# A fixed TensorE order for Layer 1 of a gated two-layer block, with ScalarE copies out of PSUM and one softmax inversion a sequence

## The chip, the core and the metric

The kernel runs on one core of a Trainium2 chip. TensorE (PE in the profile) multiplies matrices and leaves the results in PSUM, eight banks of 2 KB a partition; VectorE (DVE), ScalarE (ACT) and GpSimd (POOL) do the rest. GpSimd does not touch PSUM here. SyncE (SP) issues most of the DMAs. Each engine works through its own queue in the order in which the built program holds it, and waits at an instruction whose semaphores have not come.

The metric is the device time of one launch in microseconds (us). Lower is better.

## The reference

Eight sequences of 256 rows and 512 features, x[8, 256, 512], go through two layers. Each layer adds a gated attention and then a gated feed-forward part:

```python
x = x + tanh(g_xattn[0]) * attn0(layernorm(x), ctx, ctx)        # 16 heads of 32, causal
x = x + tanh(g_ffn[0])   * ffn0(layernorm(x))                   # ternary weights, silu(gate)*up, rms norm
x = x + tanh(g_xattn[1]) * attn1(layernorm(x), ctx)             # projections, rms-normed q and k
x = x + tanh(g_ffn[1])   * ffn1(layernorm(x))                   # 8-bit activations, ternary weights
```

What matters for this change is the softmax, `softmax(q k^T) v` for each of 16 heads over 256 keys (text context is empty at this length, so Layer 1 attends to the image context alone), and Layer 1's feed-forward part:

```python
h = rms_norm(x) * w_norm
value, gate = split(act_quant(h) @ weight_quant(w_gv).T)         # 2 x 2048 columns
u = value * silu(gate)
out = x + act_quant(u) @ weight_quant(w_out).T
```

## The kernel before, in words

**Stages.** The program has three stretches. In the first, Layer 0's weights are made ternary while the keys and values of Layer 1 are computed for all sequences and stored in DRAM, and the first two sequences go through Layer 0's attention. In the second, Layer 0's feed-forward part (`Feed0`, lines 645 to 744) runs sequence by sequence; around it are laid the attention of the later sequences, the quantizing of Layer 1's weights, and the first steps of Layer 1's attention. In the third (lines 900 to 1071) Layer 1 is finished: `Attention1` for each sequence and `Feed1` for each half of a sequence (128 rows, called first and second).

**Attention.** A sequence's 16 heads are worked in four groups of four (g = 0 to 3). `scores(g)` multiplies q by k with queries on partitions, and VectorE takes the row maxima `nm`, one reduction for each pair of heads (L329 in Layer 1). `shift` splits the negated maxima into three bf16 parts on GpSimd, turns them with TensorE (`nt`) and copies them to `nT`. `exps(g)` multiplies k by q with keys on partitions, adds the maxima by a second matmul with `sel`, and ScalarE takes the exponential in two halves, `p[1]` first (L400). `weigh(g)` multiplies p by v, and p by `ones`, into the two halves of one PSUM bank `o`; VectorE then inverts the second half (L422) and multiplies (L423), so that `oT` holds finished head outputs. Layer 1 adds the output projection `proj` (L255, reached through `done`).

**Layer 1's feed-forward part.** `norm` (a chain through VectorE and GpSimd) makes 8-bit rows `zq`, a DMA transposes them to `zT`. Each of eight `glu(k)` a half fills one of two `gu` banks with 8 matmuls (L985); ScalarE takes tanh of the first half of the bank (L993), and VectorE reads the bank twice (L994, L996). Only then is the bank free. Every second one is followed by a maximum (L998). `quantize` turns the maxima into a scale, ScalarE scales (L1020), GpSimd rounds (L1021), two DMAs transpose, and `project` multiplies by the output weights into `py` (L1035, added at L1045).

**PSUM in the third stretch.** Score and transpose tiles share a pool `s` of two tiles of two banks each; then there are one `o`, two `gu` and one `py`. Queries' projection, output projection and `project` all use `py`.

**What sets the order.** Every job is a list of steps with a time interval; `timeline` sorts the steps by these times and emits them. The tile framework then schedules each engine's queue itself, by its own model of time, within the dependencies. Inside one `scores` or `exps` the class `Row` ties each matmul behind the one before; otherwise TensorE's order is the scheduler's.

Of the kernel before, what the change touches and what calls it, by code (L numbers as in the profile page):

```python
# [47 lines left out]
P = 128  # L49
# [20 lines left out]
LAG = 2  # L70


@with_exitstack
def flamingo_kernel(
# [104 lines left out]
    for g in range(DC):  # L179
        nc.vector.tensor_copy(sel[:, g, :], chosen[:, g : g + 1].broadcast_to([P, P]))  # L180
    mz = []
    for k in range(2):
        mz.append(const.tile([P, 2, P], BF, name=f"mz{k}"))
        nc.gpsimd.memset(mz[k], 0.0)

# [31 lines left out]

    class Row:
# [4 lines left out]
        def matmul(self, *args, **kwargs):  # L223
            ins = nc.tensor.matmul(*args, **kwargs)  # L224
            if self.last is not None:
                tc.add_manual_dep(
                    ins.ins,
                    self.last.ins.name,
                    mybir.DependencyInfo(
                        mybir.DependencyClass.NoSync, mybir.DependencyReason.DATA  # L230
                    ),
                    reason="row",
                )
            self.last = ins
# [9 lines left out]
    def turned(srcs, dst):  # L244

        t = pair((P, 2, DC, P), name="turned")
        for i, src in enumerate(srcs):
            for c in range(DC):
                nc.tensor.transpose(t[:, i, c, :], src[:, c * P : (c + 1) * P], ident)  # L249
        nc.scalar.copy(dst.rearrange("p c (i t) -> p i c t", i=2), t)  # L250

    def linear(dst, srcT, i, w):

        for c in range(DC):
            nc.tensor.matmul(  # L255
# [8 lines left out]
    class Attention:  # L264
# [68 lines left out]
        def shift(self):  # L333
# [4 lines left out]
            for k in range(MP):  # L338
# [12 lines left out]
                src = rest  # L351
            t = pair((P, 2, P), BF, name="nt")
            for q in range(2):
                nc.tensor.transpose(t[:, q, :], self.mz[:, q, :], ident_b)
# [48 lines left out]
        def weigh(self, g, p):  # L403
# [3 lines left out]
            for k in range(2):  # L407
                for kb in range(2):
                    for r in range(4):
                        h = 4 * g + r  # L410
                        nc.tensor.matmul(  # L411
                            o[HD * r : HD * (r + 1), k, q0[kb] : S],
                            lhsT=ones if k else self.v[:, kb, h * HD : (h + 1) * HD],
# [5 lines left out]
            if g == 0:  # L419
                self.oT = self.new("oT", [DC, S], bufs=1)  # L420
            w = self.new("w", [S])
            nc.vector.reciprocal(w, o[:, 1, :])  # L422
            nc.vector.tensor_tensor(self.oT[:, g, :], o[:, 0, :], w, ALU.mult)  # L423

        def looks(self):
            return self.counted(
                self.nready, [*(lambda g=g: self.scores(g) for g in range(DC)), self.shift]
            )

        def step(self, g):  # L430
            before = getattr(self, "p", None)
            if g < DC:
                self.exps(g)
            if g > 0:
                self.weigh(g - 1, before)

        def weighs(self):
            return self.counted(
# [686 lines left out]
```

## Time and profile before

| | us |
|---|---|
| median of 3 timed runs | 1401.51 (1391.04 to 1401.55) |
| the profiled execution | 1398.44 |
| its span on the core | 1396.6 |
| TensorE busy | 1212.5 (87%) |
| VectorE busy | 900.2 (64%) |
| ScalarE busy | 515.9 (37%) |
| GpSimd busy | 491.0 (35%) |
| mean granted TensorE clock | 0.933 |

"Busy" is the sum of an engine's instructions in the span. A row of the costliest groups has the line, engine and operation, the tiles written and read, the shapes, how many there were, their busy time and the mean duration of one, then how long the engine stood idle before them and what ended that. Windows of the trace give the same busy times for a stretch, with the clock granted to TensorE (1.00 is full speed). The trace's time runs from the start of the span.

### The profile page before, as it was taken

How to read it: one execution, taken by the hardware profiler on the slowest of the kernel's cores; microseconds unless marked ns; L12 is line 12 of the kernel's file. 1: busy time of each engine (PE TensorE's matmuls, PEld its weight loads, DVE VectorE, ACT ScalarE, POOL GpSimd, SP SyncE). 2: the span in 40 equal slices, each digit the busy share in tenths (PEclk: the TensorE clock that was granted, in tenths of full speed). 3: DMA queues.
4: the chain of work that ended last, by engine and by line, in shares of the span. 5: the costliest groups of instructions: out<-in, count | busy, mean ns of one | idle time of the engine just before them, and what ended most of it. 6: DMA issues, size and time to landing. Idle time of an engine off the chain costs nothing.

```text
span 1396.6 us, 28443 instructions
## 1 busy us (share of the span) xinstructions
PE 1212.5 (87%) x11730; PEld 797.8 (57%) x11730; DVE 900.2 (64%) x1913; ACT 515.9 (37%) x978; POOL 491.0 (35%) x744
## 2 busy tenths in 40 slices
PE   5999964879999878999999998979797979898985
PEld 2444432657777656778777774545444545455552
DVE  2758779535656575656556464786858595868673
ACT  2445454555343313343333432323231414142432
POOL 2233242232424779142424234250505050413141
PEclk9999985979999989999999998989899998999998
DMA  6334334672100464101000013212020111111122
GB/s 233 136 129 145 128 107 153 223 196 93 27 32 17 145 208 118 32 17 32 17 32 17 2 62 109 50 31 54 23 61 17 38 43 35 42 28 27 36 46 53
DMA packets 103826, 104.34 MB, mean 75 GB/s; under 512 B 63376, under 2 KB 74640, under 8 KB 103696
## 3 DMA queue, kind: packets, MB, share of 16 engines
q1 hardware_dynamic: 100672, 97.54, 24.0%
q10 hardware_dynamic: 3024, 4.98, 1.1%
q8 instruction: 92, 1.51, 0.4%
q14 instruction: 38, 0.31, 0.1%
HBM read 72.09 MB, written 15.73 MB: 63 GB/s over the span
## 4 chain that ended last, share of the span: by engine, by line
PE 39%; DVE 20%; POOL 8%; ACT 6%; DMA 6%; issue 5%; SPq 0%; ACTq 0%; POOLq 0%; DVEq 0%
PE gu L682 9%; PE s L224 6%; PE o L411 6%; PE y L707 5%; PE gu L985 4%; PE lin L255 4%; DVE nm L329 3%; DMA w<-in_gvT_dram 2%; PE py L1035 2%; DVE ln_st L198 2%; ACT u L1020 2%; DVE t L994 2%; POOL rs_r L191 1%; POOL q L805 1%; PE turned L249 1%
## 5 line engine op out<-in xcount | busy, mean ns | idle before, releaser
L682 PE MATMUL gu<-xT,gu 128*128 128x128 f16 x4096 | 268.2, 224 | 10.0 <-DVE h L692 7.0
L682 PEld LDWEIGHTS <-gu 128*128 128x128 bf16 x4096 | 243.0, 101 | 52.2 <-issue 31.2
L985 PE MATMUL gu<-gv,zT 128*128 128x256 fp8e4 x1024 | 145.5, 292 | 38.1 <-DVE u L996 34.6
L707 PE MATMUL y<-pr,hs 128*128 128x512 f32 x512 | 157.6, 426 | 8.7 <-DVE x L740 4.3
L993 ACT ACTIVATE t<-gu,back 128x256 f32<-128x256 f32 x128 | 59.4, 471 | 262.6 <-PE gu L985 240.3
L985 PEld LDWEIGHTS <-zT 128*128 128x128 bf16 x1024 | 103.2, 104 | 92.1 <-issue 73.3
L191 POOL TENSOR_TENSOR rs_r<-rs_t,mhalf 128x1 f32<-128x1 f32 (+1 forms) x88 | 55.6, 639 | 274.9 <-DVE rs_t L189 200.8
L422 DVE RECIPROCAL w<-o 128x256 f32<-128x256 f32 x64 | 112.3, 1754 | 59.2 <-PE o L411 59.2
L699 POOL TENSOR_TENSOR acc<-acc,h 128x256 f32<-128x256 f32 x112 | 82.7, 738 | 158.0 <-ACT h L697 139.2
L400 ACT ACTIVATE p<-s 128x768 f32<-128x768 f32 (+1 forms) x128 | 109.9, 908 | 24.4 <-PE s L224 15.8
L691 DVE SCALAR_TENSOR_TENSOR h<-h,gu 128x256 f32<-128x256 f32 x128 | 53.3, 416 | 100.5 <-ACT h L690 98.9
L224 PE MATMUL s<-qT,kT 32*128 32x256 f32 (+1 forms) x1024 | 102.9, 405 | 10.2 <-ACT p L400 10.2
L707 PEld LDWEIGHTS y<-pr,hs 128*128 128x128 f32 x512 | 89.6, 196 | 24.3 <-issue 6.5
L694 ACT CAST hs<-h 128x256 fp32r<-128x256 f32 x128 | 51.6, 404 | 140.0 <-DVE h L692 139.8
L1021 POOL TENSOR_SCALAR uq<-u 128x1024 bf16<-128x1024 f32 x32 | 33.4, 1044 | 183.0 <-ACT u L1020 102.1
L1035 PE MATMUL py<-ou,uT 128*128 128x512 fp8e4 x256 | 70.3, 430 | 21.2 <-DVE x L849 12.2
L994 DVE SCALAR_TENSOR_TENSOR t<-t,gu 128x256 f32<-128x256 f32 x128 | 52.1, 413 | 55.7 <-ACT t L993 55.4
L216 POOL TENSOR_TENSOR hs<-h,hs 128x256 fp32r<-128x256 f32 x64 | 46.8, 731 | 114.7 <-ACT hs L694 114.7
L224 PE MATMUL s<-kT,qT 32*128 32x256 f32 (+1 forms) x1024 | 81.4, 393 | 6.3 <-DVE nm L329 4.3
L697 ACT ACTIVATE h<-h 128x256 f32<-128x256 f32 x112 | 46.4, 416 | 92.6 <-POOL hs L216 64.3
L690 ACT ACTIVATE h<-gu 128x256 f32<-128x256 f32 x128 | 48.2, 377 | 84.7 <-PE gu L682 79.9
L224 PEld LDWEIGHTS s<-qT,kT 32*128 32x128 f32 x1024 | 54.0, 199 | 44.4 <-issue 21.8
(142 smaller groups left out, 2133.4 us busy)
## 6 DMA issues: line engine op xcount, KB each, us to landing
w<-in_gvT_dram SPq DMA_DIRECT2D x32, 512.0 KB, 4.0
w<-in_guT_dram SPq DMA_DIRECT2D x32, 256.0 KB, 2.8
w<-in_outT_dram SPq DMA_DIRECT2D x16, 512.0 KB, 4.0
x<-in_x_dram SPq DMA_DIRECT2D x16, 256.0 KB, 5.5
cT<-in_cxT_dram SPq DMA_DIRECT2D x8, 512.0 KB, 4.8
kT<-in_cxT_dram SPq DMA_DIRECT2D x8, 512.0 KB, 4.2
v<-in_cx_dram SPq DMA_DIRECT2D x8, 512.0 KB, 4.1
vd<-v SPq DMA_DIRECT2D x8, 512.0 KB, 5.0
```

Source lines behind the costliest of these rows:

```text
L191: nc.gpsimd.tensor_tensor(r[:, :n], t[:, :n], mhalf[:, :n], ALU.pow)
L224: ins = nc.tensor.matmul(*args, **kwargs)
L400: nc.scalar.activation(self.p[j], s[j][:, :, 0:n], AF.Exp)
L411: nc.tensor.matmul(o[HD * r : HD * (r + 1), k, q0[kb] : S], lhsT=ones if k else self.v[:, kb, h * HD : (h + 1) * HD], rhs=p[r // 2][:, r % ...
L422: nc.vector.reciprocal(w, o[:, 1, :])
L682: nc.tensor.matmul(gu[:, k, half, :], lhsT=wgu[dc][:, j : j + P], rhs=self.xT[:, i, part * DC + dc, :], start=(dc == 0 and part == 0), sto ...
L699: nc.gpsimd.tensor_tensor(self.acc[i], self.acc[i], sq, ALU.add)
L707: nc.tensor.matmul(self.ys, lhsT=hs[:, part, half, :], rhs=wpr[c][:, half * D : (half + 1) * D], start=(c == 0 and half == 0 and part == 0 ...
L985: nc.tensor.matmul(gu[:, half, :], lhsT=self.zT[:, c, :], rhs=wgv[c][1 - half][:, k * S : (k + 1) * S], start=(c == 0), stop=(c == DC - 1),)
L993: nc.scalar.activation(t, gu[:, 0, :], AF.Tanh, scale=self.back[:, 1:2])
L994: nc.vector.scalar_tensor_tensor(t, t, 1.0, gu[:, 0, :], ALU.add, ALU.mult)
L1035: nc.tensor.matmul(py, lhsT=self.uT[:, c, :], rhs=wout[c // 4][:, c % 4, :], start=(c == 0), stop=(c == HC - 1),)
```

## The change

Four things are changed together.

1. **Softmax sums.** The sums' matmul takes `pick[:, g, :]` instead of `ones`: 32 columns of which only the 8 of group g are one. The sums of the four groups thus fall on different partitions and can be added into one tile. `weigh` no longer inverts or multiplies: ScalarE copies the whole bank `o` (128x512) to `oT`, and from the second group on GpSimd adds the sums. In Layer 0's `done` the sums are turned with the outputs (two more transposes a sequence), inverted as 32 numbers a row, and multiplied in. In Layer 1's `done` one inversion of 128x256 is followed by four matmuls with `spread`, which carry the inverses to all partitions, and two multiplications of 128x512; banks `o` and `py` are used in turn (for the first sequence `o` alone).
2. **The gate's bank.** ScalarE copies each `gu` bank (128x512) to SBUF tiles `gv`, and tanh and both VectorE operations read the copy.
3. **The order.** All matmuls and transposes go through a small class `Tensor`; while `held` is set, each is tied behind the one before. It is set for the third stretch alone. There the steps are placed one by one on a grid of sixteen steps a sequence, one `glu` a step.
4. **Finer steps.** `shift` is split into `parts` (GpSimd) and `shift` (TensorE), `weighs` into eight steps; `load` comes before the queries; `zT` has three buffers instead of two.

```diff
+    class Tensor:
+        held = False
+        last = None
+        def kept(self, ins):
+            if self.held:
+                self.last = behind(ins, self.last)
+            return ins
+        def matmul(self, *args, **kwargs):
+            return self.kept(nc.tensor.matmul(*args, **kwargs))
...
                         pe.matmul(
                             o[HD * r : HD * (r + 1), k, q0[kb] : S],
-                            lhsT=ones if k else self.v[:, kb, h * HD : (h + 1) * HD],
+                            lhsT=pick[:, g, :] if k else self.v[:, kb, h * HD : (h + 1) * HD],
...
-            w = self.new("w", [S])
-            nc.vector.reciprocal(w, o[:, 1, :])
-            nc.vector.tensor_tensor(self.oT[:, g, :], o[:, 0, :], w, ALU.mult)
+                self.oT = self.new("oT", [DC + 2, S], bufs=1)
+                self.sums = self.oT[:, DC, :]
+            behind = DC + (g > 0)
+            nc.scalar.copy(self.oT[:, g : behind + 1 : behind - g], o)
+            if g > 0:
+                nc.gpsimd.tensor_tensor(self.sums, self.sums, self.oT[:, behind, :], ALU.add)
...
+                    pe.transpose(sums[:, i, :], self.sums[:, rows], ident)
+                nc.vector.reciprocal(
+                    inv, sums.rearrange("p i (r g e) -> p i g r e", r=4, g=DC)[:, :, :, :, 0]
+                )
...
+            def invert():
+                nc.vector.reciprocal(self.oT[:, DC + 1, :], self.sums)
+            def divide():
+                for k in range(2):
+                    w = bank(("o", "py")[k if self.b else 0], (P, 2, S), name="inv")
+                    for j in range(2):
+                        pe.matmul(
+                            w[:, j, :],
+                            lhsT=spread[:, 2 * k + j, :],
+                            rhs=self.oT[:, DC + 1, :],
+                            start=True,
+                            stop=True,
+                        )
+                    cols = self.oT[:, 2 * k : 2 * k + 2, :]
+                    nc.vector.tensor_tensor(cols, cols, w, ALU.mult)
+            def add(i):
+                xt = xs[2 * self.b + i]
+                nc.gpsimd.tensor_tensor(xt, xt, rob, ALU.add)
+                t = bank(("o", "py")[i if self.b else 0], name="proj")
+                linear(t, self.oT, i, lambda c: wo[:, c, :])
+                nc.vector.scalar_tensor_tensor(xt, t, tg[:, 1:2], xt, ALU.mult, ALU.add)
...
+            gv = work.tile([P, 2, S], F32, tag="gv", name="gv", bufs=3)
+            nc.scalar.copy(gv, gu)
-            nc.scalar.activation(t, gu[:, 0, :], AF.Tanh, scale=self.back[:, 1:2])
-            nc.vector.scalar_tensor_tensor(t, t, 1.0, gu[:, 0, :], ALU.add, ALU.mult)
+            nc.scalar.activation(t, gv[:, 0, :], AF.Tanh, scale=self.back[:, 1:2])
+            nc.vector.scalar_tensor_tensor(t, t, 1.0, gv[:, 0, :], ALU.add, ALU.mult)
-            nc.vector.tensor_tensor(cols, t, gu[:, 1, :], ALU.mult)
+            nc.vector.tensor_tensor(cols, t, gv[:, 1, :], ALU.mult)
...
+        at(b, *((k, step) for k, step in enumerate(first.glus() + second.glus())))
+        for n, f in ((0, first), (8, second)):
+            quantize, turn0, turn1, project = f.done()
+            at(b, (n + 7.9, quantize), (n + 8.5, turn0), (n + 9, turn1), (n + 13.6, project))
+        if b >= 2:
+            norm, turn, load, lin0, lin1, scale, turn_q = a.ready()
+            at(b - 2, (-2.1, norm), (-0.8, turn), (-0.5, load))
+            at(b - 2, *(((-0.3, lin0), (-0.2, lin1)) if b == 2 else ((0.2, lin0), (1.2, lin1))))
+            at(b - 2, (1.9, scale), (3.6, turn_q))
+            s0, s1, s2, s3, parts, shift = a.looks()
+            at(b - 2, (10.2, s0), (12.2, s1), (13.2, s2), (14.2, s3), (14.9, parts))
+            at(b - 1, (2.1, shift))
         if b >= 1:
+            e0, e1, w0, e2, w1, e3, w2, w3 = a.weighs()
+            n = -0.7 if b == 1 else 2.2
+            at(b - 1, (n, e0), (n + 1, e1) if b > 1 else (n + 0.1, e1))
+            at(b - 1, (4.2, w0) if b > 1 else (n + 0.2, w0))
+            at(b - 1, (5.2, e2), (6.2, w1), (7.2, e3), (8.2, w2), (9.2, w3))
+        invert, divide, add0, add1 = a.done()
+        at(b - 1, (9.9, invert), (10.7, divide), (11.2, add0), (12.7, add1))
+        for n, f in ((11.9, first), (12.9, second)):
+            norm, turn = f.ready()
+            at(b - 1, (n, norm), (n + 1.5, turn))
+    pe.held = True
     timeline(*jobs)
```

In the built program a full sequence of the third stretch stands on TensorE in this order, with one `gate` (8 matmuls) to a step: gate 0, lin0, gate 1, lin1, gate 2, nt, e0, gate 3, e1, turn of the queries, gate 4, w0, gate 5, e2, project of the sequence before, gate 6, w1, gate 7, e3, gate 8, w2, gate 9, w3, gate 10, s0, divide, gate 11, add0, gate 12, s1, add1, gate 13, s2, project, gate 14, s3, gate 15, turn of the rows.

VectorE's queue is still the scheduler's: from the inversion on it holds the reductions of s0, the two multiplications, then mixed the gates' operations, both halves' norm chains, the layer norm of a later sequence, and the reductions of s1, s2 and s3, in this order.

## The prediction

> **What bounds the kernel now.** I read the page first (busy shares, slices), then windows of the trace cut at the last gate of each of Layer 1's sequences, then TensorE's waits in that stretch, the costliest groups, and the order in time.
>
> ```profile
> PE 1212.5 (87%) x11730; PEld 797.8 (57%) x11730; DVE 900.2 (64%) x1913; ACT 515.9 (37%) x978; POOL 491.0 (35%) x744
> ```
> ```profile
> core 0: us, PE busy (x) PEld busy (x) DVE busy (x) ACT busy (x) POOL busy (x), PEclk, DMA share, GB/s
> ...
> 200.00:239.00 39.00, 17.95 (x150) 8.11 (x150) 36.18 (x71) 21.98 (x39) 10.14 (x8) 0.63 0.44 135
> 239.00:845.00 606.00, 559.60 (x7141) 441.88 (x7140) 350.16 (x707) 232.18 (x522) 246.28 (x369) 0.95 0.25 74
> ...
> 996.40:1074.00 77.60, 63.02 (x499) 35.18 (x497) 54.12 (x113) 22.85 (x34) 25.81 (x43) 0.93 0.15 38
> 1074.00:1154.50 80.50, 67.16 (x503) 37.60 (x504) 56.40 (x116) 22.98 (x34) 25.91 (x51) 0.90 0.15 40
> ```
> ```profile
> 1046.00:1078.00 32.00, 22.52 (x151) 12.41 (x144) 30.45 (x62) 3.31 (x7) 17.83 (x33) 0.99 0.08 26
> ```
>
> TensorE is nearly full in Layer 0's body (560 of 606 us); VectorE bounds the last 39 us before it. A full sequence of Layer 1 takes 74.0 us on average: the five stretches from 926.2 to 1296.0, 70.2 + 77.6 + 80.5 + 75.0 + 66.5 = 369.8. On average none of the engines is full there, but the last row shows what an average hides: for 32 us VectorE is busy 30.5 and TensorE 22.5. That is the dense part, from the last inversion to the last score maxima.
>
> ```profile
> PE gu L985 <- DVE u L996: 34.6, 18, 6.0
> PE py L1035 <- DVE x L849: 12.2, 6, 2.4
> ```
> ```profile
> 1045.61 1.76 DVE L422 RECIPROCAL w<-o 128x256 f32<-128x256 f32 x1 [0.45 <-PE o L411]
> ...
> 1073.52 2.35 DVE L329 TENSOR_REDUCE nm<-s 128x4 f32<-128x1024 f32 x2
> ```
>
> The dense part runs from 1045.61 to 1075.87: 30.3 us of VectorE work on end. TensorE's waits (us in total, times, longest) name the same engine.
>
> **The change, part by part.**
>
> *Softmax, start and Layer 0.* Each weighing loses an inversion and a multiplication and gains a copy:
>
> ```profile
> L422 DVE RECIPROCAL w<-o 128x256 f32<-128x256 f32 x64 | 112.3, 1754 | 59.2 <-PE o L411 59.2
> ```
>
> With 0.42 us for L423, 2.18 us go, 8.7 a sequence; Layer 0's end gives back 2 x 0.69 us (128x512 multiplications like L557, 691 ns) and a small inversion. ScalarE's copy of 128x512 lies by the cast of the same size (L537, 579 ns), 0.59 us; it has 22 of 39 us filled at the start. The second sequence's four weighings lie in the 39 us that VectorE bounds: 0 to 8.7 us, I take -6, since a quantizing job ends that stretch. In the body TensorE waits 46 us, about 29 of it for VectorE; against that, 6 x 3 GpSimd sums of 0.74 us (L699) and two more transposes a sequence. Bounds -10 to +8; I take -2, most waits being at handovers.
>
> *Handover.* Divide and both projections of the first sequence share the one bank `o`: matmul, multiply, matmul, multiply, project, add, project in series, where before a single projection started the norm. About 3.5 us later at the first norm; lin0, lin1 and a weighing are done meanwhile: +3.
>
> *The gate's bank.* The copy frees a bank 0.59 us after the last matmul, where before tanh (0.47) and two VectorE operations (2 x 0.42, in VectorE's queue) had to end. The 34.6 us of waits for L996 look like the prize. But 8 of these us are in the last sequence; the long ones (4.75, 5.97, 5.11) stand at the end of the dense part, where TensorE now waits for VectorE elsewhere. In the last sequence it is a gain: 16 gates at 1.25 us and two projects, 27 us against 32: -5. ScalarE gets 16 x 0.59 + 4 x 0.59 = 11.8 us a sequence, on 22.9 of 75.
>
> *The fixed order of a full sequence.* From the order in the program and the trace's times I walk one period. TensorE's groups, start to start at full clock: gate 0.90 x16, lin and add 3.54 x4, project 3.48 x2, exps 1.28 x4, weighings 1.87 x4, scores 1.08 x4, two turns 1.9, nt 0.25; new are the four divide matmuls, each shown as two passes, half the columns of a projection in all: 1.8. Sum 56.
>
> - *w3.* ScalarE's queue has half of e3's exponentials, then quantize's two scalings, which wait for gate 7's maximum, then the other half, gate 8's copy and tanh, and w2's copy, which frees `o`. From gate 7's end: copy and tanh 1.1, VectorE 1.6 + 1.0, scalings 2.37, exponential 1.0, copy, tanh, copy 1.65, together 8.8 us with the hand-offs. TensorE has e3, gate 8, w2 and gate 9: 4.95. Wait 3.9.
> - *Inversion.* After w3 a copy (0.6) and GpSimd's sum (0.74): 1.5 us until VectorE can start.
> - *Dense part.* Its list in VectorE's queue is that of before, less 0.42 (L423), plus two multiplications (1.38) and the add of `project` (0.75), which now stands ahead of s3's maxima: 30.3 + 1.7 = 32.0. The turn of the rows is behind s3's maxima in the pool `s`, so TensorE cannot pass it; its own work in this part is 21.2.
> - *From the turn to e3.* 27.9 us of work; nT 0.4, e1 behind e0's exponentials 1.1, the queries' turn behind both of e1's 2.1.
>
> Period: 6.8 + 3.9 + 1.5 + 32.0 + 27.9 + 3.6 = 75.7, at full clock and without new contention.
>
> *Clock.* The walk has pauses of 3.9 (w3), about 2.6 (s3) and 5 (turn).
>
> ```profile
> 1132.90:1135.30 2.40, 0.03 (x1) 0.00 (x0) 2.19 (x8) 0.47 (x1) 0.60 (x4) 1.00 0.00 0
> 1135.30:1138.70 3.40, 3.38 (x9) 1.29 (x9) 3.40 (x12) 0.00 (x0) 0.53 (x1) 0.53 0.19 39
> ```
>
> A pause of 2.4 us was followed by 3.4 us at about half clock. The Trainium skill (TensorE: Matmul & The Clock Gate, "HAM oscillation") asks for no idle gaps over some 3.4 us. By the rule two pauses cost, by the row three; half clock for 3.4 to 6.8 us loses 1.7 to 3.4 us each, but in the dense part TensorE has slack. I charge w3 1.7 and the turn 2.6: 4.3.
>
> *Two SBUF inputs.* Both VectorE operations of a gate had one input in PSUM (at most 423 ns each); now both lie in SBUF. L216's VectorE form, two SBUF inputs of the same size, has a median of 425 ns, but a mean of 476 and a maximum of 1044. The skill (SBUF — State Buffer, "SBUF: two separate sides") says that such an operation and a GpSimd instruction lock each other out for a whole instruction. By the row ten operations in the dense part cost 0.6 us; by the rule, with GpSimd busy 17.8 of 32 us and an estimated half of its 0.8 us left at each meeting, 2.2. I take 1.0.
>
> A full sequence: 75.7 + 4.3 + 1.0 = 81.0, 7.0 more than before; five: +35. The first stretch has the same dense part but no lin, e0 and e1: +3. The sixth has no scores: +4. The end after the last gate stays 18.6.
>
> Sum: -6 - 2 + 3 + 3 + 35 + 4 - 5 = +32. The profiled execution's own time is 1398.4 (span 1396.6, 1.8 around it), 3.1 below the median of the timed runs; 1398.4 + 32 = 1430.4. I say 1430.
>
> Edits at no cost: `pick` for `ones` has the same shape; `load` earlier and `zT`'s third buffer add no work on a filled queue (SP's transposes follow their norms; were `zT` late, gate 0 would wait out a transpose, some 3 us: a pair took 6.48); parts split from shift stays GpSimd work, 2.8 us before nt, behind two adds of 1.27 us and hidden by lin0 and lin1; uncovered it would hold nt for 5.3.
>
> **The rivals.**
>
> *The order keeps TensorE fed (faster).* The place is w3 and the e-phase: if quantize's scale is ready before e3's exponentials, the 3.9 and 3.6 us go, and with shorter pauses most of the half clock: 75.7 - 7.5 + 1 = 69 a sequence, -25 in all; with -6, -6, +3, -2, 0, -5 that is -41, 1357. It decides at 74 - 8/5, about 72 a sequence. For it: before, TensorE ran 20 us windows without a pause. Against it: the two scalings stand between the exponentials in ScalarE's queue, whoever is early.
>
> *The two halves cancel (no change).* If half clock and locks cost no more than before (74 holds 5 us of half clock already, its waits included), a period is 76 and Layer 0 gains 8: 1398 + 10 + 5 - 8 - 5, about 1400.
>
> *Half clock stays (much slower).* If each of the three pauses brings 6.8 us of half clock onto the path and the locks reach 2.2: 75.7 + 9 + 2.2 = 87, +65 and the rest: 1460.
>
> *The order isn't what it says.* The built program has the sixteen steps; little chance.
>
> **How the numbers follow.** Likeliest (1430, its own range 1415 to 1448): 0.50. Fed: 0.20. Cancel: 0.18. Much slower: 0.12. Changes under 1% can't be told from none here. Range 1365 to 1456; faster 0.20, same 0.18, slower 0.62.
>
> **What would show it.** Right: full sequences of about 80 us; a wait of TensorE before w3 for ScalarE's copy of `o` of some 4 us; the turn of the rows waiting for L329's successor about 5 us; VectorE without a pause for 32 us or more; clock at 0.9. Wrong: sequences under 72 us, a clock near 1.00, or w3 without a wait. I would be wrong too if Layer 0's body, whose order the scheduler has made anew, moved by more than 10 us.

## The result, and the profile after

The changed kernel takes **1452.66 us** (median; 1450.09 to 1453.91) against 1399.83 (1391.04 to 1401.55) for the kernel before in the same session: a ratio of **1.0388, 95% interval 1.0341 to 1.0435**. It is slower. The forecast was 1430 with a range of 1365 to 1456; its sum said +32, and the span of the profiled execution grew by 54.0, from 1396.6 to 1450.6 us. The measured time lies 3.3 us inside the upper end of the range and above the 1415 to 1448 that the prediction gave to its own account.

The page's row of busy times of the changed kernel:

```profile
PE 1226.9 (85%) x11810; PEld 813.8 (56%) x11810; DVE 827.1 (57%) x1837; ACT 626.0 (43%) x1170; POOL 535.9 (37%) x797
```

VectorE lost 73 us of work (900.2 before) and ScalarE took 110 more (515.9 before). TensorE's 80 extra matmuls and its slower clock come to 14 us; the other 40 are time in which TensorE stands. To see where, I cut both spans at the same events (the end of Layer 0's last sum of squares, the start of the first gate half of Layer 1, the end of the last gate half of each sequence):

| stage | before, us | after, us | difference | predicted |
|---|---|---|---|---|
| start and Layer 0, to its last sum of squares | 845.8 | 839.4 | -6.4 | -8 |
| handover, to the first gate half | 19.8 | 47.2 | **+27.4** | +3 |
| first stretch | 60.6 | 53.4 | -7.2 | +3 |
| five full sequences | 369.6 | 387.7 | +18.1 | +35 |
| sixth stretch | 50.4 | 60.7 | +10.3 | +4 |
| last sequence's gates | 32.0 | 43.4 | **+11.4** | -5 |
| tail | 18.4 | 18.8 | +0.4 | 0 |
| sum | 1396.6 | 1450.6 | +54.0 | +32 |

The sign was right and the total lay in the range, but five of the seven terms were off, in both directions. The same stages of the changed kernel by windows (stretch and its length, then busy us and count of each engine, granted TensorE clock, DMA share, GB/s):

```profile
core 0: us, PE busy (x) PEld busy (x) DVE busy (x) ACT busy (x) POOL busy (x), PEclk, DMA share, GB/s
199.00:238.40 39.40, 19.61 (x210) 9.47 (x207) 28.51 (x60) 25.10 (x44) 12.23 (x11) 0.76 0.43 135
238.40:839.40 601.00, 554.33 (x7136) 442.03 (x7135) 304.94 (x677) 246.26 (x548) 262.01 (x390) 0.96 0.25 74
839.40:886.60 47.20, 32.17 (x128) 15.06 (x129) 14.85 (x41) 6.20 (x8) 21.60 (x28) 0.75 0.26 81
1019.90:1097.50 77.60, 65.52 (x507) 38.08 (x506) 50.27 (x107) 35.04 (x54) 27.98 (x45) 0.90 0.15 39
1097.50:1174.70 77.20, 62.99 (x507) 36.97 (x506) 50.20 (x106) 34.62 (x54) 25.02 (x42) 0.92 0.17 37
...
1388.00:1431.20 43.20, 28.69 (x160) 17.50 (x158) 25.66 (x63) 20.14 (x37) 8.70 (x11) 0.76 0.19 43
```

VectorE no longer fills the stretch ahead of Layer 0's body (28.5 of 39.4 us, 36.2 of 39 before), yet Layer 0's body starts only 0.9 us earlier (238.4 instead of 239.3 us): the work taken off VectorE did not come off its length. What ends it now was not tested. In the two full sequences ScalarE is busy 35 us instead of 23, and VectorE 50 instead of 55. Three of the rows have a slow clock, but the start and the handover had one before too (0.63 and 0.74); only at the end is it new, 0.76 where it was 0.95.

TensorE's waits over the five full sequences of the changed kernel (940 to 1327 us; what waited, for what, total, times, longest):

```profile
PE turned L210 <- DVE nm L358: 22.7, 5, 6.7
PE o L207 <- ACT oT L456: 17.4, 5, 3.6
PE s L207 <- DVE rs_t L217: 7.1, 4, 1.8
PE py L207 <- DVE x L922: 6.2, 5, 1.3
PE turned L210 <- ACT p L432: 5.2, 5, 1.0
PE inv L207 <- DVE oT L901: 4.0, 5, 1.3
```

The gates' wait for VectorE is gone from the list. Before it was, in these five sequences:

```profile
PE gu L985 <- DVE u L996: 26.7, 10, 6.0
```

In its place stand the two waits that the prediction had named: the turn of the rows behind the score maxima (4.5 us a sequence, about 5 predicted) and the fourth weighing behind ScalarE's copy (3.5, 3.9 predicted).

The handover of the changed kernel in order of time (start, us, engine, operation; in brackets the idle time before it and what ended it):

```profile
844.95 6.75 PE L207 MATMUL proj<-wo,oT 128*128 128x512 f32 x8 [0.78 <-DVE oT L915]
852.62 3.70 PE L207 MATMUL proj<-wo,oT 128*128 128x512 f32 x8 [0.92 <-DVE x L922]
...
860.99 0.42 DVE L1041 TENSOR_SCALAR zq<-z 128x512 bf16<-128x512 f32 x1
...
864.36 1.51 POOL L239 TENSOR_SCALAR y<-x,ln_mv,rs_r 128x512 f32<-128x512 f32 x2
...
865.18 1.97 PE L210 MATMUL turned<-ident,y 128*128 128x128 f32 x8 [8.86 <-POOL y L239]
...
886.63 1.91 PE L207 MATMUL gu<-gv,zT 128*128 128x256 fp8e4 x16
```

The quantized rows `zq` for the first gate half are done at 861.4, and only their transposing DMA is left. But the order puts the turn of another sequence's rows first, and those rows are normed on GpSimd behind both norm chains: TensorE stands for 8.86 us. Behind the turn stand two steps of exponents, a weighing and both projections; the gate half starts at 886.63. The first projection ran at a granted clock of 0.54 after the waits ahead of it, 6.75 us for the eight matmuls that take 3.70 a moment later.

The end of the changed kernel, in order of time:

```profile
1404.87 6.59 PE L207 MATMUL py<-ou,uT 128*128 128x512 fp8e4 x16 [4.56 <-DMA uT<-uq]
1424.97 5.09 PE L207 MATMUL py<-ou,uT 128*128 128x512 fp8e4 x16 [5.44 <-DVE umax L1082]
1441.53 5.34 PE L207 MATMUL py<-ou,uT 128*128 128x512 fp8e4 x16 [9.72 <-DMA uT<-uq]
```

The first two of these projections wait for their transposed input while gate matmuls of the last sequence stand behind them in the fixed order. (The row of the second names VectorE's maximum, which ended just then; the transpose for it was issued at 1421.68 and takes some 3.2 us to land.) Before, the same two projections stood among the last gates as well, but late enough to wait for nothing:

```profile
1357.01 3.62 PE L1035 MATMUL py<-ou,uT 128*128 128x512 fp8e4 x16
...
1373.15 4.24 PE L1035 MATMUL py<-ou,uT 128*128 128x512 fp8e4 x16
```

### The profile page after: what moved, and what is told of

It is laid out like the page before. It is cut to its first block, busy times and chain, and to the rows that moved or that the text cites. A ratio compares the mean times of both kernels' runs of the same rounds, so it can differ in the third digit from the quotient of the medians.

```text
span 1450.6 us, 28745 instructions
## 1 busy us (share of the span) xinstructions
PE 1226.9 (85%) x11810; PEld 813.8 (56%) x11810; DVE 827.1 (57%) x1837; ACT 626.0 (43%) x1170; POOL 535.9 (37%) x797
## 4 chain that ended last, share of the span: by engine, by line
PE 45%; DVE 17%; ACT 8%; POOL 6%; DMA 5%; issue 3%; ACTq 0%; POOLq 0%; DVEq 0%; SPq 0%
PE gu L207 15%; PE s L207 6%; PE o L207 6%; PE y L207 5%; PE lin L207 4%; DVE nm L358 3%; PE proj L207 3%; PE py L207 3%; DMA w<-in_gvT_dram 2%; ACT p L432 2%; PE turned L210 2%; ACT u L1104 2%; DVE t L1078 1%; DVE ln_st L226 1%; DMA w<-in_outT_dram 1%
## 5 line engine op out<-in xcount | busy, mean ns | idle before, releaser
L207 PE MATMUL gu<-xT,gu 128*128 128x128 f16 x4096 | 269.0, 225 | 17.9 <-DVE h L749 13.2
L1075 ACT COPY gv<-gu 128x512 f32<-128x512 f32 x128 | 74.0, 582 | 203.0 <-PE gu L207 202.9
L207 PE MATMUL y<-pr,hs 128*128 128x512 f32 x512 | 154.2, 422 | 2.7 <-POOL hs L244 2.0
L1078 DVE SCALAR_TENSOR_TENSOR t<-t,gv 128x256 f32<-128x256 f32 x128 | 60.8, 477 | 124.0 <-ACT t L1077 122.8
L459 POOL TENSOR_TENSOR oT<-oT 128x256 f32<-128x256 f32 x48 | 37.9, 789 | 164.7 <-ACT oT L456 164.5
L207 PE MATMUL s<-qT,kT 32*128 32x256 f32 (+1 forms) x1024 | 91.8, 395 | 3.9 <-ACT p L432 3.6
L207 PE MATMUL o<-p,v 128*32 128x256 f32 (+1 forms) x1024 | 67.3, 373 | 26.0 <-ACT oT L456 26.0
L207 PE MATMUL py<-ou,uT 128*128 128x512 fp8e4 x256 | 64.1, 408 | 27.2 <-DMA uT<-uq 14.3
L358 DVE TENSOR_REDUCE nm<-s 128x4 f32<-128x1024 f32 x64 | 76.1, 1216 | 0.5 <-PE s L207 0.5
L207 PE MATMUL lin<-wk,cT 128*128 128x512 f32 x128 | 60.3, 616 | 16.9 <-DMA cT<-in_cxT_dram 16.9
```

The lines of the kernel that those rows point to most:

```text
L207: return self.kept(nc.tensor.matmul(*args, **kwargs))
L358: nc.vector.tensor_reduce(nm, s[j].rearrange("p r (q k) -> p r q k", q=2), AX.X, ALU.max, negate=True)
L459: nc.gpsimd.tensor_tensor(self.sums, self.sums, self.oT[:, behind, :], ALU.add)
L1075: nc.scalar.copy(gv, gu)
L1078: nc.vector.scalar_tensor_tensor(t, t, 1.0, gv[:, 0, :], ALU.add, ALU.mult)
```

## The experiments

The ratios are to the kernel before, timed in the same session (its medians there: 1396.2 for the first four runs, 1395.2 for the next four, 1398.5 for the three after them, 1397.3 for the last). None leaves out a part of the reference. The question was whether the loss comes from the fixed order, from ScalarE's copy or from the new softmax; then, which places of the order; then, whether they add up.

### The order not held

```diff
-    pe.held = True
     timeline(*jobs)
```

> The changed kernel with the hold taken off: the sixteen-step placing stays as the order in which the steps are given out, but TensorE's order is the scheduler's again. Theory (the fixed order costs: gate 0 stands behind 20 us of held work at the handover, and a weighing, the scores and a turn wait in place with all of TensorE behind them): most of the 53 us goes, 1395 to 1420. Rival (the added work costs: ScalarE's copies, GpSimd's sums, divide, and VectorE operations with two SBUF inputs): stays at 1440 or more.

Measured: 1401.95 us, ratio 1.0041 (1.0024 to 1.0058). The same steps on the same grid, with the new softmax and the copy, but TensorE's queue left to the scheduler, cost 51 us less than with the order held. The handover is 22.6 us and the five full sequences 351.4, shorter than before (369.6). Behind them the time is lost again: the sixth stretch, the last gates and the tail take 124.6 us, 100.8 before. What is left of waits in the full sequences is above all TensorE waiting for the gates' transposed input, over 925 to 1273 us:

```profile
PE gu L207 <- DMA zT<-zq: 33.5, 5, 8.8
```

So nearly the whole loss needs the held order. It doesn't follow that holding is bad, only that this order, held, is.

### The new softmax alone

The kernel before with its own job list and gates read from PSUM. Of the change it has the once-a-sequence inversion and, with it, the finer steps of `shift`, `weighs` and `done`; what these steps do alone was not tried.

```diff
-            w = self.new("w", [S])
-            nc.vector.reciprocal(w, o[:, 1, :])
-            nc.vector.tensor_tensor(self.oT[:, g, :], o[:, 0, :], w, ALU.mult)
+            nc.scalar.copy(self.oT[:, g : behind + 1 : behind - g], o)
```

> The kernel before with the softmax part alone (copy of the bank o by ScalarE, sums added by GpSimd, one inversion a sequence, divide), the old jobs and times, gates read from PSUM, no hold. Theory: the start and Layer 0's body keep the 6.5 us that the changed kernel gained there, and Layer 1 gains a little from 5.6 us less VectorE work a sequence: 1375 to 1396. Rival (the added copies, sums and divide matmuls cost): 1405 to 1425.

Measured: 1415.71 us, ratio 1.0137 (1.0108 to 1.0167). This was a miss. The 7 us up to the end of Layer 0 are there (838.7 us against 845.8), but late in Layer 1 they are lost, above all in one sequence of 91.6 us (74.8 the one before it). Two windows of this kernel, mostly an ordinary sequence and mostly that one, and two pieces of the second:

```profile
1136.00:1212.00 76.00, 67.03 (x506) 38.11 (x506) 46.19 (x105) 24.67 (x38) 23.64 (x39) 0.91 0.15 39
1212.00:1302.00 90.00, 75.57 (x508) 41.90 (x508) 48.15 (x110) 24.96 (x38) 30.13 (x53) 0.83 0.10 23
...
1217.91:1234.98 17.07, 15.07 (x78) 9.54 (x82) 9.01 (x23) 6.84 (x10) 7.40 (x13) 0.50 0.22 42
1272.52:1286.17 13.65, 12.22 (x33) 6.40 (x34) 8.56 (x10) 0.00 (x0) 0.00 (x0) 0.50 0.12 23
```

The number of matmuls is nearly the same and TensorE is busy 8.5 us longer, at a mean clock of 0.83: after a pause of 4.17 us for `zT` and one of 3.87 for the inversion it had half clock for 17.1 and 13.7 us, mostly busy. So less work on VectorE didn't make the kernel faster: the scheduler's new order has other pauses. Which job's place brings these two was not tried and stays open.

### The new softmax with the copy

```diff
+            gv = work.tile([P, 2, S], F32, tag="gv", name="gv", bufs=3)
+            nc.scalar.copy(gv, gu)
```

> As the run before, and the gate's bank copied to SBUF as well; old jobs, no hold. Theory: the copy frees a gate bank earlier, in the dense part VectorE stays the bound: within 8 us of the softmax part alone, either way. Rival (two SBUF inputs and 9.4 us more ScalarE work a sequence cost): 12 us or more above it.

Measured: 1420.92 us, ratio 1.0171 (1.0144 to 1.0198): 5 us more than without the copy. With the scheduler free the copy takes the gates' wait for VectorE away, 26.4 us in 926 to 1302 without it, and a wait for `zT`, 24.5 us, takes its place.

### The fixed order without the copy

```diff
-            gv = work.tile([P, 2, S], F32, tag="gv", name="gv", bufs=3)
-            nc.scalar.copy(gv, gu)
```

> The changed kernel, fixed order and all, with the gates read from PSUM again, without the copy. Theory: one gate a step leaves a bank two steps to come free, so the copy buys nothing there; the third weighing's wait loses the two copies ahead of it (1.2 us of 3.6) and VectorE the locks (2 us a sequence): 1438 to 1452. Rival A (the copy is the main cost): 1425 or less. Rival B (the copy is what lets the fixed order run): 1465 or more.

Measured: 1439.26 us, ratio 1.0301 (1.0267 to 1.0336). Within the fixed order the copy costs 13 us, a quarter of the loss. The two large waits stay, 18.3 and 15.8 us over the five sequences against 22.7 and 17.4: most of each is there without the copy.

### One layer norm earlier

```diff
-            at(b - 2, (-2.1, norm), (-0.8, turn), (-0.5, load))
+            at(b - 2, (-6.5 if b == 2 else -2.1, norm), (-0.8, turn), (-0.5, load))
```

> The changed kernel with one thing moved: at the handover the layer norm of the later sequence is issued at -6.5 steps instead of -2.1, so it stands ahead of the softmax chain in VectorE's and GpSimd's queues. Theory A (the held order makes TensorE stand behind whatever it meets first; at the handover that is 8.86 us for GpSimd's y in front of the turn): the 8.86 us wait goes, the handover falls from 47 to about 38 us, the run is 1440 to 1447 us. Rival B (TensorE's handover is bounded by the chain of projections at a slow clock and by the softmax chain, so that the wait only moves to the next held step): within 3 us of 1452.7.

Measured: 1442.25 us, ratio 1.0327 (1.0285 to 1.037): 10.4 us less. The turn now follows the projection at once, the wait of 8.86 us is gone, and the handover is 37.4 instead of 47.2 us. The wait was loss, as the first theory said; it didn't move to the next step.

### The scaling behind the copies of o

```diff
-            at(b, (n + 7.9, quantize), (n + 8.5, turn0), (n + 9, turn1), (n + 13.6, project))
+            at(b, (n + 9.3, quantize), (n + 9.4, turn0), (n + 9.5, turn1), (n + 13.6, project))
...
-                    nc.scalar.activation(u, u, AF.Identity, bias=magic, scale=sc)
+                    behind(nc.scalar.activation(u, u, AF.Identity, bias=magic, scale=sc), copied[0])
```

`copied[0]` is the last copy of `o` by ScalarE; the scaling is only tied behind it in ScalarE's queue.

> The changed kernel with ScalarE's scaling of the gated products issued behind the copies of o instead of ahead of them (and the turns behind it moved by the same amount). Theory A (the fixed order costs by its waits, and the 17.4 us in front of o over five sequences is ScalarE still scaling): the wait of 3.0 to 3.6 us a sequence in front of the later windows goes, 1428 to 1438 us. Rival B (VectorE's dense stretch of gate multiplications sets the sequence's length, so the wait only moves to the turn or the projection): within 5 us of 1452.7.

Measured: 1419.91 us, ratio 1.0166 (1.013 to 1.0201): 32.7 us less, more than expected. TensorE's waits over 935 to 1300 us of this kernel:

```profile
PE turned L210 <- DVE nm L360: 19.6, 5, 6.7
PE s L207 <- DVE rs_t L217: 6.8, 4, 1.8
PE py L207 <- DVE x L924: 6.7, 5, 1.7
PE inv L207 <- DVE oT L903: 6.5, 5, 1.3
```

The wait for the copy of `o` is gone, and none has taken its place (the inverses' grew by 2.5 us, the turn's fell by 3.1). The five full sequences take 362.5 us instead of 387.7: 25 us for a wait of 17.4. (The other 7 us came outside them, 4.9 in the first stretch and 2.5 in the sixth.) From one turn of the rows to the next, four periods on average, it is 72.4 us instead of 77.5: 37.4 instead of 41.2 up to the fourth weighing, 3.5 instead of 4.1 from there to the inversion (the weighing now runs at a quicker clock), 31.5 instead of 32.1 from there to the turn. So the pause cost itself and about half as much again. This is the largest single place of the loss.

### No special placing at the handover

```diff
-            at(b - 2, (-2.1, norm), (-0.8, turn), (-0.5, load))
-            at(b - 2, *(((-0.3, lin0), (-0.2, lin1)) if b == 2 else ((0.2, lin0), (1.2, lin1))))
+            at(b - 2, (-2.1, norm), (0.1 if b == 2 else -0.8, turn), (0.15 if b == 2 else -0.5, load))
+            at(b - 2, (0.2, lin0), (1.2, lin1))
...
-            n = -0.7 if b == 1 else 2.2
-            at(b - 1, (n, e0), (n + 1, e1) if b > 1 else (n + 0.1, e1))
-            at(b - 1, (4.2, w0) if b > 1 else (n + 0.2, w0))
+            at(b - 1, (2.2, e0), (3.2, e1), (4.2, w0))
```

> The changed kernel without its special placing at the handover: the first gate half comes ahead of the earlier sequence's sums and of the later sequence's projections there, as in the other sequences. Theory A (the first gate half is ready some 20 us before TensorE gets to it, and stands behind the held work): gate 0 starts near 866 us instead of 886.6, the handover shrinks to 22 to 28 us, some 13 to 15 us of the displaced work comes back in the first sequence; net 1442 to 1448 us. Rival B (the displaced work comes back in full, since TensorE has to do it before the second sequence anyway): 1450 to 1455 us.

Measured: 1447.61 us, ratio 1.0362 (1.0324 to 1.04): 5.0 us less. Its handover and first stretch:

```profile
841.20:863.90 22.70, 11.11 (x24) 4.66 (x23) 10.52 (x33) 0.00 (x0) 14.51 (x19) 0.84 0.46 161
863.90:934.00 70.10, 59.77 (x488) 34.78 (x488) 44.96 (x92) 31.28 (x50) 24.46 (x32) 0.93 0.11 27
```

The first gate half starts at 863.9, 23 us earlier, and 16.7 us come back in the first stretch. Handover and first stretch together are 92.8 us here, 100.6 in the changed kernel, 89.9 with the early layer norm and 80.4 before. So some 17 of the handover's 27.4 us were work done early, not loss. The loss of the two stages together is 20.2 us, and the early layer norm takes half of that away.

### The last projections later

```diff
-(n + 13.6, project))
+(n + (16.5 if (b, n) in ((B - 2, 8), (B - 1, 0)) else 13.6), project))
```

> The changed kernel with the last projections but one placed later: those of the seventh sequence's second half and of the eighth's first half at step 16.5 instead of 13.6, so that the gate matmuls of the last sequence stand ahead of them. Theory A (at the end TensorE stands in front of projections, 4.56 and 5.44 us, with ready gate matmuls behind them): 1442 to 1445 us. Rival B (the end is bounded by VectorE's last multiplications and the transposes behind them, so that what is taken out of the wait comes back in the last one, 9.72 us): within 3 us of 1452.7.

Measured: 1441.98 us, ratio 1.0325 (1.0286 to 1.0365): 10.7 us less. The last sequence's gates take 30.5 us instead of 43.4, at a clock of 0.89 instead of 0.76, and the tail behind them 21.0 instead of 18.8:

```profile
1385.90:1416.40 30.50, 21.05 (x146) 15.01 (x144) 22.88 (x59) 19.58 (x36) 8.66 (x11) 0.89 0.30 59
```

This is below the 32.0 us of before; the prediction had worked out 27.

### The four moves together

The four edits above in one kernel; where two of them touch the same line:

```diff
-            at(b - 2, (-2.1, norm), (-0.8, turn), (-0.5, load))
+            at(b - 2, (-6.5 if b == 2 else -2.1, norm), (0.1 if b == 2 else -0.8, turn), (0.15 if b == 2 else -0.5, load))
```

> The changed kernel with the four moves together: the layer norm of the first held turn early, the scaling behind the copies of o, no special placing at the handover, the last projections later. Theory A (the held order's cost is a sum of separate waits, each of which can be taken out by itself): the two moves at the handover overlap and give 10 to 15 us, the others 33 and 11 as measured alone, so 1393 to 1400 us. Rival B (behind each wait the next one is nearly due, so that the gains don't add): 1408 to 1420 us.

Measured: 1407.65 us, ratio 1.0058 (1.0043 to 1.0073). The gains sum to 53.8 us with the larger of the two at the handover, and 45.0 came, at the very edge of the second expectation. By the ratios to the kernel before the sum is 3.46% and 3.30% came, so how much is missing is not sure. Where gains don't add is the handover: it and the first stretch are 93.2 us, against 92.8 without the special placing alone and 93.4 with the later scaling alone, so the early layer norm brought nothing there, where its turn no longer stands in front. The five full sequences are 363.2 us, as with the later scaling alone (362.5).

### The turn of the rows later

```diff
-            at(b - 2, (-6.5 if b == 2 else -2.1, norm), (0.1 if b == 2 else -0.8, turn), (0.15 if b == 2 else -0.5, load))
-            at(b - 2, (0.2, lin0), (1.2, lin1))
-            at(b - 2, (1.9, scale), (3.6, turn_q))
+            at(b - 2, (-6.5 if b == 2 else -2.1, norm), (0.7, turn), (0.75, load))
+            at(b - 2, (1.2, lin0), (1.7, lin1))
+            at(b - 2, (1.9, scale), (4.6, turn_q))
```

> The kernel with the four moves, and besides the transposes of the next sequence's normed rows placed 1.5 steps later (step 0.7 of the next sequence instead of 0.8 steps before its start), with its projections after them. Theory A (these transposes stand in front of the first gate half and wait 4 to 5 us a sequence for VectorE to read the scores' banks; placed behind that gate half they find the banks free): the 19.6 us over five sequences goes, and ScalarE's wait for them too; 15 to 25 us below the kernel with the four moves. Rival B (the wait is only passed on, to the projections or to the gate half behind them, because VectorE is late by the same amount): within 5 us of the kernel with the four moves.

Measured: 1401.52 us, ratio 1.0025 (1.0014 to 1.0035): 6.1 us less, hardly more than the rival's 5. The wait of the turn for the maxima is still 18.1 us over five sequences (19.5 with the four moves). One gate half in front of it, about 1 us of matmuls, is no cover: the turn still waits 3.6 us a sequence. The first theory was wrong here.

### The same without the copy

```diff
-            gv = work.tile([P, 2, S], F32, tag="gv", name="gv", bufs=3)
-            nc.scalar.copy(gv, gu)
```

> The kernel with the four moves and the later transposes, but the gates read from PSUM as before the change (no copy by ScalarE). Theory A (the copy costs by ScalarE's queue, 13 us of the changed kernel's time as measured with its order): 5 to 15 us faster than the same kernel with the copy. Rival B (with TensorE's waits gone the copy's early release of the gate bank and VectorE's shorter multiplications, 48 us busy in a sequence against 54, begin to pay): 5 to 20 us slower than with the copy.

Measured: 1394.42 us, ratio 0.9978 (0.9962 to 0.9993): 7.1 us less than with the copy. TensorE's waits over 925 to 1285 us, the five largest:

```profile
PE gu L207 <- DVE u L1080: 16.4, 7, 4.8
PE py L207 <- DVE x L924: 8.3, 5, 2.0
PE inv L207 <- DVE oT L903: 6.5, 5, 1.3
PE s L207 <- DVE nm L360: 4.6, 4, 1.2
PE lin L207 <- DVE lin L616: 4.3, 5, 0.9
```

The turn's wait has fallen to 2.6 us and the gates' wait for the multiplications has come back with 16.4: the same late VectorE, met at another step. In this order the copy moves the wait, it doesn't remove it, and it costs ScalarE's time besides.

### The steps spread

```diff
-            at(b - 2, (-6.5 if b == 2 else -2.1, norm), (0.7, turn), (0.75, load))
-            at(b - 2, (1.2, lin0), (1.7, lin1))
-            at(b - 2, (1.9, scale), (4.6, turn_q))
+            at(b - 2, (-6.5 if b == 2 else -8.5, norm), (-0.3 if b == 2 else 0.7, turn), (0.75, load))
+            at(b - 2, (1.2, lin0), (2.05, lin1))
+            at(b - 2, (2.06, scale), (4.6, turn_q))
-            at(b - 2, (10.2, s0), (12.2, s1), (13.2, s2), (14.2, s3), (14.9, parts))
+            at(b - 2, (10.2, s0), (11.6, s1), (12.6, s2), (13.6, s3), (14.3, parts))
-            at(b - 1, (2.2, e0), (3.2, e1), (4.2, w0))
+            at(b - 1, (2.2 if b > 1 else -0.2, e0), (3.2, e1), (4.2, w0))
-        at(b - 1, (9.9, invert), (10.7, divide), (11.2, add0), (12.7, add1))
+        d = 0.5 if 0 < b < B - 1 else 0
+        at(b - 1, (9.9, invert), (10.7 + d, divide), (11.2 + 2 * d, add0), (12.7 + d, add1))
```

The norms of the two halves move by `d` too, and the first half's projection goes from step 13.6 to 14.6.

> The kernel with the four moves, the later transposes and no copy, and six more small moves in its fixed order: the next sequence's layer norm 6.4 steps earlier, its second projection behind a gate half, three of its four score steps 0.6 steps earlier, the inverses' spreading and the output projections half a step to a step later with a gate half in between, the first gate projection of a sequence one step later, and one step of exponents in front of the first gate half at the handover. Theory A (what TensorE still waits for, 49.5 us in 925 to 1285 us, is mostly a step standing too close behind VectorE's, and a gate half in between hides it): the waits in front of the inverses, the projections and the scores, some 28 us, mostly go, 1365 to 1380 us. Rival B (VectorE's dense stretch at the end of a sequence sets the pace, and each wait is passed on to the next gate half): 1388 to 1400 us.

Measured: 1368.15 us, ratio **0.9791 (0.9761 to 0.982)**: 26.3 us less than the run before, and 2.1% faster than the kernel before the change. TensorE's waits over 925 to 1262 us:

```profile
PE py L207 <- DVE x L924: 13.2, 5, 2.8
PE gu L207 <- DVE u L1080: 12.5, 7, 2.6
PE s L207 <- DVE nm L360: 2.3, 5, 0.5
PE inv L207 <- DVE oT L903: 1.6, 5, 0.3
PE s L207 <- DVE nT L390: 1.2, 5, 0.2
PE s L207 <- ACT p L434: 1.1, 5, 0.2
```

The waits in front of the projections and their rows are gone, that of the inverses has fallen from 6.5 to 1.6 us and the scores' from 7.4 to 4.6. The project's wait for the output's add has grown from 8.3 to 13.2, so part was passed on. In all they fell from 49.5 to 31.9, and the five full sequences from 357.4 to 340.7 us, with TensorE's busy time the same (308.7 and 308.5). The rest came in the first stretch (57.1 instead of 64.8) and in the sixth (53.1 instead of 57.2). The five full sequences and the sixth stretch of this kernel:

```profile
922.30:1263.00 340.70, 308.50 (x2533) 178.92 (x2532) 236.45 (x522) 124.86 (x190) 122.74 (x207) 0.97 0.16 40
1263.00:1316.10 53.10, 46.37 (x410) 28.04 (x408) 32.28 (x83) 21.74 (x32) 16.45 (x31) 0.97 0.18 33
```

The five take 340.7 us where the kernel before took 369.6 with a clock of 0.93 and VectorE busy 265.1. So a held order can be faster than the scheduler's orders here, once fewer of its steps stand close behind VectorE. Whether VectorE's lighter load is needed for it isn't shown: no held order was run with the old softmax. Since six moves were made at once, their single shares aren't known, and neither is what this kernel would do with the copy or with the order not held.

## Why the prediction was right, and where its sum was not

**Right as worked out.** The weighing's copy, 0.58 us (0.59 assumed). The three named waits: 3.5 us a sequence before the fourth weighing (3.9), 4.5 before the turn (about 5), and the third, of the queries' turn, 1.0 where 2.1 was assumed. The cost of the two SBUF inputs: the rows of the changed kernel

```profile
L1075 ACT COPY gv<-gu 128x512 f32<-128x512 f32 x128 | 74.0, 582 | 203.0 <-PE gu L207 202.9
...
L1078 DVE SCALAR_TENSOR_TENSOR t<-t,gv 128x256 f32<-128x256 f32 x128 | 60.8, 477 | 124.0 <-ACT t L1077 122.8
```

show 477 ns where L994 took 413, and L1080 takes 422 where L996 took 414: sixteen times 0.064 and 0.008 is 1.15 us a sequence, against 1.0 taken. In the last run, which reads PSUM again, the first is 417.

**Right in the sum and wrong in its parts: the start and Layer 0.** Together they gave -6.4 against -8. But of the 6 us at the start, in the stretch that VectorE seemed to bound, 0.9 came, and the body, from which 2 were taken, is 5.5 shorter. Over all kernels here with the new softmax the body takes 599.8 to 606.1 us, 606.5 before, so how much of the 5.5 is the softmax and how much the scheduler's new order stays open. That the sum came out is luck.

**The dense part was right in length.** From the inversion to the maxima that the turn waits for, in order of time:

```profile
1068.98 1.75 DVE L901 RECIPROCAL oT<-oT 128x256 f32<-128x256 f32 x1 [1.43 <-POOL oT L459]
...
1101.11 2.35 DVE L358 TENSOR_REDUCE nm<-s 128x4 f32<-128x1024 f32 x2
```

To the turn at 1102.47 it is 33.5 us; over four sequences 30.7, 33.5, 33.5 and 30.7, mean 32.1, with 32.0 predicted. The period from turn to turn is 76.5, 79.3, 77.7 and 76.5, mean 77.5. The walk gave 75.7 at full clock: 40.3 from the turn to the fourth weighing (41.2 measured), 3.4 from there to the inversion (4.1), and the 32.0.

**A term that came out small by cancelling: clock and locks in a full sequence.** On the 75.7 the prediction charged 4.3 for half clock and 1.0 for locks, and the period came out 1.8 longer than the walk. But from the turn to the fourth weighing the walk had waits of 7.5 us, and the trace has 4.7 (3.5 for the copy of `o`, 1.0 for the queries' turn, 0.2 for exponentials). Against these 2.8 stands the slow clock. The time just behind a pause in front of the weighing, and the time around two turns (clock in the third column from the right):

```profile
1065.00:1068.00 3.00, 3.00 (x35) 1.39 (x36) 1.87 (x4) 1.32 (x3) 0.93 (x1) 0.69 0.73 178
...
1018.36:1028.60 10.24, 6.95 (x27) 4.66 (x26) 9.23 (x23) 3.20 (x5) 8.42 (x19) 0.50 0.13 38
1093.45:1107.11 13.66, 8.53 (x38) 5.88 (x39) 11.33 (x19) 2.98 (x5) 9.15 (x20) 0.50 0.10 29
```

Half clock begins ahead of the turn, where VectorE's list sets the time and TensorE has slack; the dense part does not get longer by it (32.1 against 32.0). Behind the turn it goes on for 3.4 to 5.4 us, in which TensorE has no pause: an estimated 2.3 us a sequence, half of their mean, where 2.6 were charged. Behind the weighing's pause the way to the inversion is 0.7 longer (4.1 against 3.4), where 1.7 were charged. Something over 1 us before the fourth weighing is not accounted for. That a full sequence takes 77.5 and not 81.0 us is 17 us over five.

**The step that failed: "lin0, lin1 and a weighing are done meanwhile: +3" at the handover.** It took for granted that TensorE does that work while it waits. The order is fixed, and the first thing in it is the turn, which needs GpSimd's `y`; the prediction costed the chain to the first norm and never asked when the first *held* step has its input. The early layer norm, which takes 10.4 us off, shows this. That the displaced work is missing from the first stretch (-7.2 against +3) covers 10 us of the 24; the two stages together missed by 14.2.

**The second step that failed: the last sequence as "a gain: -5".** That the gates could be quicker than before was right, if not by so much (30.5 against 32.0 once the projections are out of the way, with 27 predicted). But the walk went through a full sequence and not through the end, where a projection that still waits for its input stands in front of gates that are ready. Placing two of them later gave back 10.7 us.

**The sixth stretch** was +10.3 against +4. It holds waits of 4.5 us for the parts of the maxima and 3.0 for the copy of `o`:

```profile
1327.70:1388.40 60.70, 49.97 (x410) 29.29 (x407) 34.12 (x84) 30.95 (x48) 16.93 (x31) 0.89 0.16 29
```

TensorE is busy 50.0 us in it against 46.9 before. That is the clock rather than more work: the last run does the same 410 matmuls in 46.4 us at 0.97, and takes 53.1 us for the stretch. The other held orders take 57 to 63.

**The rival on the other side** set its place at the fourth weighing and the exponents. That place was the right one: one move there gave 32.7 us. Its condition (the scale ready before the exponentials) wasn't met, because ScalarE's queue had the scalings in between, as the argument against it said.

**The total** lay in the range in part by luck: terms that were too low by 49 us in all stood against others that were too high by 27. The rival of a much slower kernel had the nearer number, 1460, but from sequences of 87 us, and they took 77.5. (Its 87 is itself a little low: three times 3.4 us lost to half clock is 10.2, not 9.)

## What to carry to other kernels

An order that is held turns every late input into a loss for all that stands behind it, so walk it step by step through its irregular places, the first and the last sequence above all, and ask of each step when its input is ready and what ready work stands behind it. Where a step sits close behind another engine's, put independent work in between; a pause that was removed brought about its own length here (9.9 us of handover for 8.9, 16.7 of five sequences for 17.6), and in one place half as much again (25 for 17.4).

## What I had not expected of the hardware

The handover's first projection took 6.75 us and the second 3.70 for the same eight matmuls, after pauses of only 2.69 and 0.78 us close together. In the run with the new softmax alone TensorE worked without a pause from 1273.95 us on and was still at half clock 12.2 us later, after a pause of 3.87; behind the weighing's pause of 3.60 in the changed kernel half clock lasted 3.4 us. And the length of a pause alone does not tell the clock behind it: after 3.60 us in front of the weighing the next 3 us had 0.69, while a pause of 3.29 in front of the turn had 0.50 on both sides, during the pause already.
